# Expert tiles with standing weights: gate and up weights copied by ScalarE, hidden tile made already turned

## The chip, the cores and the metric

The kernel runs on one core of one Trainium2 chip. The metric is the device time of one launch in microseconds, the median of the runs shown.

## The reference

Two transformer layers on 8 sequences of 512 tokens of 256 features, all in float32. Only the last part, a mixture of experts, matters here. Each of the 4096 tokens goes to 4 of 32 experts, chosen by a router; an expert has 128 hidden units:

```python
gate_vals = silu(einsum('th,eih->tei', tokens, gate_w))     # gate_w: 32 x 128 x 256
up_vals = einsum('th,eih->tei', tokens, up_w)
hidden_vals = gate_vals * up_vals
expert_out = einsum('tei,ehi->teh', hidden_vals, down_w)    # down_w: 32 x 256 x 128
sel = take_along_axis(expert_out, topk_idx[:, :, None], axis=1)
mixed = (sel * topk_w[:, :, None]).sum(1)
```

A shared expert and the token itself are added.

## The kernel before

The kernel computes an expert only for the tokens that chose it. Earlier stages (attention of both layers, the first feed-forward, the router) end by scattering each token's row, with its weight and its place, into a table in DRAM that is sorted by expert. The table is cut into pages of 128 rows, one expert a page. All the expert weights wait in SBUF, in `store`, 768 columns per expert: 512 of gate and up (for each half `k` of the 256 features 128 of gate, then 128 of up), then 256 of down.

`pages_of(0, SURE, between)` runs over 136 pages, called expert tiles here, with index `s`. It is written under a manual schedule: each engine executes its instructions in the order of the program, and semaphores between engines are placed by dependencies. One step of the loop does, in this order:

- `fetch(s + 8)`: a DMA on SyncE's queue that brings the rows of a later tile, `r` (L1528).
- `spread(s + 3)`: two TensorE transposes of the rows, `ptr` (L1546), and a VectorE copy out of PSUM to `rT` (L1548).
- `expert_hidden(s + 2)`: the gate and up matmuls `pge` (L1554), with `rT` standing and 256 weight columns per half of the features moving; silu on ScalarE, `acte` (L1558); the product on VectorE, `hide` (L1560), tokens on partitions.
- `turned_hidden(s + 1)`: a transpose of `hide`, `pth` (L1565), and a VectorE copy to `hidT` (L1567).
- `result(s)`: the down matmul `poe` (L1572), with `hidT` standing and 256 columns of `store` moving; ScalarE scales it by the token's weight on its way out of PSUM, `y` (L1574); GpSimd scatters it to DRAM (L944).
- `each(s)`, which is `between`: for finished halves of a sequence pair it issues gathers `z` of four results per token and the VectorE additions (L1602, L1604) into `sums`, spread over 12 of every 16 steps. The last half's additions come three to a step.

Before every eighth tile, `numbers` loads eight experts' numbers from SBUF into registers (L1534), from which TensorE finds the weights in `store`. The number of the buffers of a tag is `bufs`; PSUM has eight banks, two for each of four uses.

After the loop, `rest` holds further pages under conditions that are not taken here, and `complete` gathers and adds the last half and writes it.

Of the kernel before, what the change touches and what calls it, by code (L numbers as in the profile page):

```python
# [12 lines left out]
F32 = mybir.dt.float32  # L13
I32 = mybir.dt.int32
U32 = mybir.dt.uint32
AF = mybir.ActivationFunctionType
ALU = mybir.AluOpType
AX = mybir.AxisListType
PSUM = bass.MemoryType.PSUM
DRAM = bass.MemoryType.DRAM  # L20

P = 128
B, S, H = 8, 512, 256
NT = S // P
NK = H // P
# [781 lines left out]
def _halves(x, u):  # L807

    h, p = divmod(u, B // 2)
    return [x[2 * p + r][:, 2 * h + t, :] for r in range(2) for t in range(2)]  # L810
# [54 lines left out]
def _l1(nc, tc, a, x, out, ident, mhalf, rows, results, filled, inputs, early):  # L865
# [14 lines left out]
    with ExitStack() as ctx:  # L880
        pool = lambda name, bufs, **kw: ctx.enter_context(tc.tile_pool(name=name, bufs=bufs, **kw))
# [14 lines left out]
        for half in range(2):  # L896
            s = slice(half * P, (half + 1) * P)
# [43 lines left out]
        def scatter(group, to, index, source, last):  # L941


            ins = nc.gpsimd.indirect_dma_start(  # L944
                to, bass.IndirectOffsetOnAxis(ap=index, axis=0), source, None, bounds_check=last
            )
            tc.declare_no_dep(ins.ins, group=group, reason="rows are distinct")
            tc.add_to_no_dep_group(group, ins.ins)
            if group == "results":
                tc.declare_no_dep(ins.ins, group="gathers", reason="rows gathered are finished")  # L950
            if group == "rows":
                after(ins, filled)
            scattered[group].append(ins)
            return ins
# [28 lines left out]
        q, k, v, xlT = {}, {}, {}, {}  # L983
        prods, sums, sc, softs, values, turned = {}, {}, {}, {}, {}, {}
# [495 lines left out]
        start = [sum(T[:u]) for u in range(U + 1)]  # L1480
# [17 lines left out]
        store = keep.tile([P, NE, 3 * H], F32, tag="store", name="store")  # L1498
# [20 lines left out]
        routing.close()  # L1519
        tp = pool("m_t", 2)  # L1520
        ps_r = pool("m_psr", 2, space=PSUM)
        ps_t = pool("m_pst", 2, space=PSUM)
        ps_e = pool("m_pse", 2, space=PSUM)
        ps_y = pool("m_psy", 2, space=PSUM)

        def fetch(s):
            r = tp.tile([P, ROW], F32, tag="r", name="r", bufs=TILES + 3)
            ins = nc.sync.dma_start(r, rows[s * P : (s + 1) * P, :])  # L1528
            after(ins, scattered["rows"][-16:])
            return r  # L1530

        def numbers(s):

            _, found = nc.values_load_multi_w_load_instructions(  # L1534
                number[0:1, s : s + 8],
                [mybir.EngineType.PE],
                min_val=0,
                max_val=NE - 1,
                skip_runtime_bounds_check_because="all but the bits of an expert's number are masked out",
            )  # L1540
            return dict(enumerate(found, s))

        def spread(r):
            pt = ps_r.tile([P, S], F32, tag="psr", name="ptr")
            for k in range(NK):
                nc.tensor.transpose(pt[:, k * P : (k + 1) * P], r[:, k * P : (k + 1) * P], ident)  # L1546
            rT = tp.tile([P, H], F32, tag="rT", name="rT", bufs=3)
            nc.vector.tensor_copy(rT, pt[:, :H])  # L1548
            return rT

        def expert_hidden(w, rT):
            pg = ps_e.tile([P, S], F32, tag="pse", name="pge")
            for k in range(NK):
                nc.tensor.matmul(  # L1554
                    pg[:, :H], rT[:, k * P : (k + 1) * P], w[:, k * H : (k + 1) * H], start=k == 0, stop=k == NK - 1
                )
            act = tp.tile([P, P], F32, tag="acte", name="acte", bufs=3)
            nc.scalar.activation(act, pg[:, :P], AF.Silu)  # L1558
            hid = tp.tile([P, P], F32, tag="hide", name="hide", bufs=3)
            nc.vector.tensor_tensor(hid, act, pg[:, P : 2 * P], ALU.mult)  # L1560
            return hid

        def turned_hidden(hid):
            pt = ps_t.tile([P, S], F32, tag="pst", name="pth")
            nc.tensor.transpose(pt[:, :P], hid, ident)  # L1565
            hidT = tp.tile([P, P], F32, tag="hidT", name="hidT", bufs=3)
            nc.vector.tensor_copy(hidT, pt[:, :P])  # L1567
            return hidT

        def result(w, r, hid):  # L1570
            po = ps_y.tile([P, S], F32, tag="psy", name="poe")
            nc.tensor.matmul(po[:, :H], hid, w[:, 2 * H :], start=True, stop=True)  # L1572
            y = tp.tile([P, H], F32, tag="y", name="y", bufs=8)
            nc.scalar.activation(y, po[:, :H], AF.Copy, scale=r[:, H + 1 : H + 2])  # L1574
            scatter("results", results, r[:, H : H + 1].bitcast(U32), y, NTOK * TOPK + NS * P - 1)

        z, sums_of = {}, {}
# [17 lines left out]
        def add(u, t, part):  # L1595

            w, x_t = z[u, t], _halves(x, u)[t]
            if t == 0 and part == 0:
                sums_of[u] = tp.tile([P, NT, H], F32, tag="sums", name="sums", bufs=3)
            to = sums_of[u][:, t, :]  # L1600
            if part == 0:
                nc.vector.tensor_tensor(w[:, :2, :], w[:, :2, :], w[:, 2:, :], ALU.add)  # L1602
            else:
                nc.vector.tensor_tensor(to, x_t if part == 1 else to, w[:, part - 1, :], ALU.add)  # L1604
# [14 lines left out]
        def finish(b, s, last):  # L1619

            sent = scattered["results"][-16:]
            for t in range(NT):
                beside.setdefault(s + 2 + t if last else s + 3 + 3 * t, []).append(partial(gather, b, t, sent))
                for part in range(3):
                    beside.setdefault(s + 5 + 2 * t if last else s + 8 + 3 * t + part, []).append(
                        partial(add, b, t, part)
                    )
            for r in range(2):
                beside.setdefault(s + 8 + 4 * r if last else s + 22 + r, []).append(partial(put, b, (r,)))

        weights = lambda s: store[:, bass.ds(which[s], 1), :].rearrange("p e c -> p (e c)")
        which = {}

        def pages_of(first, end, each):

            tiles, rTs, made, hidTs = {}, {}, {}, {}
            ahead = min(TILES, end - first)
            for s in range(first, first + ahead):
                tiles[s] = fetch(s)
            for s in range(first - 3, end):  # L1640
                if first <= s < end - ahead:
                    tiles[s + ahead] = fetch(s + ahead)
                if s + 3 < end:
                    rTs[s + 3] = spread(tiles[s + 3])
                if first <= s + 2 < end:
                    if (s + 2) % 8 == 0:
                        which.update(numbers(s + 2))
                    made[s + 2] = expert_hidden(weights(s + 2), rTs.pop(s + 2))
                if first <= s + 1 < end:
                    hidTs[s + 1] = turned_hidden(made.pop(s + 1))  # L1650
                if s >= first:
                    result(weights(s), tiles.pop(s), hidTs.pop(s))
                    each(s)

        def between(s):
# [7 lines left out]
        def rest(s):  # L1663

            with tc.If(filled_rows > s * P):
                with tc.manual_schedule():
                    pages_of(s, s + 8, lambda _: None)
                if s + 8 < NS:
                    rest(s + 8)
# [14 lines left out]
        with tc.manual_schedule():  # L1684
            pages_of(0, SURE, between)
            for s in sorted(beside):
                for f in beside[s]:
                    f()
        rest(SURE)

        def complete(units):

            last = [(u, t) for u in units for t in range(NT)]
            for n in range(-4, len(last)):
                if n >= 0:
                    for part in range(3):
                        add(*last[n], part)
                    put(*last[n], nc.scalar)
                if n + 4 < len(last):
                    gather(*last[n + 4], None)  # L1700
# [147 lines left out]
```

## Time and profile before

| | |
|---|---|
| median of 3 runs | 2006.84 us (2006.36 to 2014.84) |
| the profiled execution | 2012.53 us, span 2010.7 us |
| TensorE busy in the span | 1887.2 us (94%) |
| VectorE, ScalarE, GpSimd busy | 1369.8, 1087.6, 1095.5 us |
| mean granted TensorE clock | 0.975 |
| the expert tiles | from 1759 to 1989 us of the span |

Engines are named PE (TensorE's matmuls), PEld (its weight loads), DVE (VectorE), ACT (ScalarE), POOL (GpSimd) and SP (SyncE). A timeline row gives the start in the span, the time to the end of the last of its instructions, the engine, the line, the operation, the tiles (out<-in, names without buffer numbers), the array's rows and columns, the shape and the count; in brackets stands the engine's idle time before it and what ended that. In a windows table, each column is an engine's busy time in that stretch with its instructions in parentheses, then the granted clock (1.00 is full), the mean busy share of the DMA engines and what they moved. A program's f32 matmul appears as two PE instructions, each with a weight load; a transpose as one. A matmul's shown duration includes its way through the array, so that successive ones overlap; the distance of their starts is what a series of them costs.

### The profile page before, as it was taken

To read this page: it belongs to the slowest core of one execution; us is meant where nothing else is said; L and a number is where in the kernel's file an instruction comes from. 1 tells how busy PE (TensorE), PEld (TensorE's weight loads), DVE (VectorE), ACT (ScalarE), POOL (GpSimd) and SP (SyncE) were. 2 spreads that over 40 slices of the span, in tenths; PEclk is the share of its full clock that TensorE was granted. 3 is DMA by queue.
4 is the path that set the end of the run, shared out by engine and by line. 5 is a ranking of instruction groups with operands and counts; after the bars stand their busy time and mean duration, and the time that the engine had idled before them with its cause. 6 is when DMAs were issued, how large, how long until landed. Compare 5 with 4: busy or idle time off the path is not lost. (4 is left out here: it accounts for less than half of the span.)

```text
span 2010.7 us, 48841 instructions
## 1 busy us (share of the span) xinstructions
PE 1887.2 (94%) x17824; PEld 1292.1 (64%) x17824; DVE 1369.8 (68%) x3675; ACT 1087.6 (54%) x2320; POOL 1095.5 (54%) x1294
## 2 busy tenths in 40 slices
PE   7999999999999999999999999989899886899995
PEld 4666676666667666666666666646556544488884
DVE  4677777777777777776777555346887687356666
ACT  3777677777777777777762221235444333144442
POOL 4666786867868678676783110100444444455553
PEclk9999999999999999999999999999999998799998
DMA  8999999999999999999993434910111112747887
GB/s 294 318 310 288 293 297 300 299 298 304 294 304 311 295 306 296 303 283 297 298 311 116 141 121 139 131 21 0 44 44 47 52 49 89 289 150 232 249 259 242
DMA packets 383060, 438.07 MB, mean 218 GB/s; under 512 B 42849, under 2 KB 364385, under 8 KB 382305
## 3 DMA queue, kind: packets, MB, share of 16 engines
q1 hardware_dynamic: 368608, 398.17, 64.7%
q0 software_dynamic: 12672, 35.14, 4.8%
q8 instruction: 146, 2.39, 0.5%
q10 hardware_dynamic: 1536, 1.57, 0.2%
q14 instruction: 98, 0.79, 0.1%
HBM read 235.75 MB, written 199.05 MB: 216 GB/s over the span
## 5 line engine op out<-in xcount | busy, mean ns | idle before, releaser
L448 DVE CUSTOM_DVE_ANT_0 e<-sc,winc 128x512 f32<-128x512 f32 x512 | 333.2, 689 | 280.2 <-PE sc L434 156.6
L451 ACT ACTIVATE e<-e,low 128x512 f32<-128x512 f32 x512 | 365.6, 715 | 96.8 <-DVE low L448 95.7
L372 ACT COPY strip<-pa 128x512 f32<-128x512 f32 x512 | 275.2, 591 | 129.0 <-POOL winc L402 59.2
L375 POOL TENSOR_TENSOR own<-aside,strip 128x512 f32<-128x512 f32 x256 | 269.0, 1051 | 124.9 <-ACT strip L372 108.2
L465 DVE COPY et<-et_ps 128x512 f32<-128x512 f32 x512 | 328.4, 683 | 0.8 <-PE et_ps L462 0.8
L422 PE MATMUL sc<-sm,sm 32*128 32x256 f32 (+3 forms) x1792 | 310.0, 436 | 1.0 <-DVE low L448 0.8
L365 PE MATMUL pa<-pos,sm 32*128 32x256 f32 x2048 | 291.9, 401 | 0.1
L944 POOL DMA_INDIRECT rows<-pay,slot x128 | 148.7, 1162 | 210.7 <-issue 156.8
L402 POOL TENSOR_TENSOR winp<-winp,own 128x256 f32<-128x256 f32 x256 | 187.7, 733 | 98.1 <-DMA winp<-shift 76.2
L422 PEld LDWEIGHTS sc<-sm,sm 32*128 32x128 f32 x1792 | 164.5, 184 | 98.0 <-DVE et L465 35.3
L434 PE MATMUL sc<-ident,winp 128*128 128x128 f32 x1280 | 203.2, 286 | 24.7 <-DMA winp<-shift 24.3
L402 POOL TENSOR_TENSOR winc<-winc,own 128x256 f32<-128x256 f32 x256 | 187.2, 731 | 57.9 <-DMA winc<-shift 46.4
L434 PEld LDWEIGHTS sc<-ident,winp 128*128 128x128 f32 x1280 | 137.1, 142 | 102.4 <-issue 58.3
L944 POOL DMA_INDIRECT results<-y,r x136 | 133.3, 980 | 105.0 <-ACT y L1574 54.7
L462 PE MATMUL et_ps<-ident,e 64*128 64x64 f32 x4096 | 184.4, 230 | 1.1 <-DVE et L465 1.1
L365 PEld LDWEIGHTS pa<-pos,sm 32*128 32x128 f32 x2048 | 176.1, 185 | 10.9 <-ACT strip L372 3.9
L59 POOL TENSOR_TENSOR rstd<-var,mhalf 128x2 f32<-128x2 f32 (+1 forms) x56 | 47.2, 844 | 243.4 <-DVE var L57 235.0
L462 PEld LDWEIGHTS et_ps<-ident,e 64*128 64x128 f32 x4096 | 149.1, 140 | 44.2 <-issue 22.2
L474 PE MATMUL ctx_ps<-et,v 128*32 128x128 f32 x4096 | 167.7, 282 | 0.5 <-DVE et L465 0.5
L1554 PE MATMUL pge<-store,rT 128*128 x544 | 141.3, 382 | 3.1 <-DVE rT L1548 1.4
L739 ACT ACTIVATE hT<-ph,b 128x512 f32<-128x512 f32 x64 | 44.0, 687 | 165.6 <-PE ph L736 165.6
L175 PE MATMUL pq<-xnT,wqk 128*128 128x512 f32 x256 | 132.7, 643 | 0.7 <-PE pv L157 0.7
(227 smaller groups left out, 3200.6 us busy)
## 6 DMA issues: line engine op xcount, KB each, us to landing
shift<-strip SPq DMA_DIRECT2D x256, 510.0 KB
winp<-shift SPq DMA_DIRECT2D x128, 384.0 KB
winc<-shift SPq DMA_DIRECT2D x128, 384.0 KB
winp<-shift SPq DMA_DIRECT2D x128, 256.0 KB
winc<-shift SPq DMA_DIRECT2D x128, 256.0 KB
rows<-empty SPq DMA_DIRECT2D x8, 2640.0 KB
r<-rows SPq DMA_DIRECT2D x136, 132.0 KB
z<-results SPq DMA_DIRECT2D x32, 512.0 KB
```

The lines of the kernel that those rows point to most:

```text
L365: nc.tensor.matmul(pa[:, t * W : (t + 1) * W], src[rs, i * P : (i + 1) * P], pos[rs, g, :], start=True, stop=True)
L372: nc.scalar.copy(st[:, 2 * j : 2 * j + 2, :].rearrange("p t w -> p (t w)"), pas[j])
L375: nc.gpsimd.tensor_tensor(own, aside.unsqueeze(2).to_broadcast([P, 2, 2, P]), st[:, :, W - 1 : W].rearrange("p (j t) o -> p t j o", t=2).t ...
L402: nc.gpsimd.tensor_tensor(dst, dst, own[:, t], ALU.add)
L422: nc.tensor.matmul(sc[:, c0:c1], s[side_][rs, cut : cut + P], s[2 + side_][rs, c0:c1], start=c0 == 0, stop=False, skip_group_check=True,)
L434: nc.tensor.matmul(sc[:, m * P : (m + 1) * P], wins[n + 2 * (m - i)][1][:, j, (i - m + 1) * P : (i - m + 2) * P], ident, start=False, stop ...
L448: nc.vector.tensor_tensor_reduce(e, sc, wins[n][0][:, j, :], 1.0, -LOW, ALU.add, ALU.min, low)
L451: nc.scalar.activation(e, e, AF.Exp, bias=low, scale=-1.0, accum_out=totals[b, g // 2][:, i, r : r + 1])
L462: nc.tensor.transpose(bank[:, c : c + 64], e[rs, m * P : (m + 1) * P], ident[rs, rs])
L465: nc.vector.tensor_copy(et[:, f].rearrange("p j m q -> p (j m q)"), bank)
L474: nc.tensor.matmul(ctx_ps[32 * r : 32 * r + 32, i * P : (i + 1) * P], vs[b % 2][:, m, g % 2, g // 2 * 4 + r, :], et[:, :, m, :], start=m = ...
L944: ins = nc.gpsimd.indirect_dma_start(to, bass.IndirectOffsetOnAxis(ap=index, axis=0), source, None, bounds_check=last)
```

## The change

Gate and up change places with the rows: the weights stand and `rT` moves, so that `pge` comes out with hidden units on partitions, as the down matmul wants it. `turned_hidden` goes, with its PSUM pool and its VectorE copy. The standing weights are no longer addressed in `store` by a register: `brought`, called four tiles ahead and first in the step, has ScalarE copy the 512 columns of the tile's expert into a fixed buffer `w` (one of four). The numbers are now loaded into registers of TensorE (for the down weights) and of ScalarE (for the copies). Results of odd tiles are scaled out of PSUM by VectorE, those of even tiles by ScalarE as before. `y` has 6 buffers instead of 8, `sums` 2 instead of 3, `pge` and `poe` three PSUM banks each instead of two.

```diff
-        ps_t = pool("m_pst", 2, space=PSUM)
-        ps_e = pool("m_pse", 2, space=PSUM)
-        ps_y = pool("m_psy", 2, space=PSUM)
+        ps_e = pool("m_pse", 3, space=PSUM)
+        ps_y = pool("m_psy", 3, space=PSUM)
...
-                [mybir.EngineType.PE],
+                [mybir.EngineType.PE, mybir.EngineType.Activation],
...
         def expert_hidden(w, rT):
             pg = ps_e.tile([P, S], F32, tag="pse", name="pge")
-            for k in range(NK):
-                nc.tensor.matmul(
-                    pg[:, :H], rT[:, k * P : (k + 1) * P], w[:, k * H : (k + 1) * H], start=k == 0, stop=k == NK - 1
-                )
+            for half in range(2):
+                for k in range(NK):
+                    nc.tensor.matmul(
+                        pg[:, half * P : (half + 1) * P],
+                        w[:, k * H + half * P : k * H + (half + 1) * P],
+                        rT[:, k * P : (k + 1) * P],
+                        start=k == 0,
+                        stop=k == NK - 1,
+                    )
...
-        def turned_hidden(hid):
-            pt = ps_t.tile([P, S], F32, tag="pst", name="pth")
-            nc.tensor.transpose(pt[:, :P], hid, ident)
-            hidT = tp.tile([P, P], F32, tag="hidT", name="hidT", bufs=3)
-            nc.vector.tensor_copy(hidT, pt[:, :P])
-            return hidT
-
-        def result(w, r, hid):
+        def brought(s):
+            w = tp.tile([P, 2 * H], F32, tag="w", name="w", bufs=4)
+            nc.scalar.copy(w, store[:, bass.ds(which[s], 1), : 2 * H].rearrange("p e c -> p (e c)"))
+            return w
+
+        def result(s, w, r, hid):
             po = ps_y.tile([P, S], F32, tag="psy", name="poe")
             nc.tensor.matmul(po[:, :H], hid, w[:, 2 * H :], start=True, stop=True)
-            y = tp.tile([P, H], F32, tag="y", name="y", bufs=8)
-            nc.scalar.activation(y, po[:, :H], AF.Copy, scale=r[:, H + 1 : H + 2])
+            y = tp.tile([P, H], F32, tag="y", name="y", bufs=6)
+            if s % 2:
+                nc.vector.tensor_scalar(y, po[:, :H], r[:, H + 1 : H + 2], None, ALU.mult)
+            else:
+                nc.scalar.activation(y, po[:, :H], AF.Copy, scale=r[:, H + 1 : H + 2])
...
-            for s in range(first - 3, end):
+            for s in range(first - 4, end):
+                if s + 4 < end:
+                    if (s + 4) % 8 == 0:
+                        which.update(numbers(s + 4))
+                    brings[s + 4] = brought(s + 4)
                 if first <= s < end - ahead:
                     tiles[s + ahead] = fetch(s + ahead)
-                if s + 3 < end:
+                if first <= s + 3 < end:
                     rTs[s + 3] = spread(tiles[s + 3])
                 if first <= s + 2 < end:
-                    if (s + 2) % 8 == 0:
-                        which.update(numbers(s + 2))
-                    made[s + 2] = expert_hidden(weights(s + 2), rTs.pop(s + 2))
-                if first <= s + 1 < end:
-                    hidTs[s + 1] = turned_hidden(made.pop(s + 1))
+                    made[s + 2] = expert_hidden(brings.pop(s + 2), rTs.pop(s + 2))
                 if s >= first:
-                    result(weights(s), tiles.pop(s), hidTs.pop(s))
+                    result(s, weights(s), tiles.pop(s), made.pop(s))
                     each(s)
```

More of the change, by code (lines that the diff above doesn't have):

```diff
@@ L1598, in add @@
             if t == 0 and part == 0:
-                sums_of[u] = tp.tile([P, NT, H], F32, tag="sums", name="sums", bufs=3)
+                sums_of[u] = tp.tile([P, NT, H], F32, tag="sums", name="sums", bufs=2)
             to = sums_of[u][:, t, :]
@@ L1634, in pages_of @@
         def pages_of(first, end, each):
-            tiles, rTs, made, hidTs = {}, {}, {}, {}
+            tiles, rTs, made, brings = {}, {}, {}, {}
             ahead = min(TILES, end - first)
```

## The prediction

> **What bounds the kernel now.** I read the page's slices first, then the groups of the last 250 us, then one period of the timeline. The change touches only the loop over expert tiles, which starts when the first fetched rows land, at 1759 us, and ends with the last result at 1989. The busy time by windows shows which engine carries it:
>
> ```profile
> core 0: us, PE busy (x) PEld busy (x) DVE busy (x) ACT busy (x) POOL busy (x), PEclk, DMA share, GB/s
> 1757.00:1764.00 7.00, 6.06 (x29) 4.09 (x28) 2.20 (x7) 0.79 (x3) 0.00 (x0) 1.00 0.69 207
> 1764.00:1985.00 221.00, 218.35 (x1188) 181.60 (x1187) 142.08 (x468) 98.74 (x264) 128.55 (x132) 1.00 0.74 227
> 1985.00:2010.70 25.70, 3.48 (x16) 2.13 (x14) 12.90 (x29) 2.45 (x6) 4.74 (x5) 0.66 0.64 228
> ```
>
> TensorE is busy in 218 of 221 us, at the full granted clock; no other engine passes two thirds, and the DMA engines stand at 0.74. A busy TensorE is not proof of a bound, because the ends of matmuls are modelled. So the starts decide, in one period of the timeline:
>
> ```profile
> 1800.55 0.27 PE L1565 MATMUL pth<-ident,hide 128*128 128x128 f32 x1
> 1800.55 0.30 PEld L1572 LDWEIGHTS poe<-store,hidT 128*128 128x128 f32 x2
> 1800.65 0.60 PE L1572 MATMUL poe<-store,hidT 128*128 x2
> 1801.09 0.38 PE L1546 MATMUL ptr<-ident,r 128*128 128x128 f32 x2
> 1801.20 0.73 PEld L1554 LDWEIGHTS pge<-store,rT 128*128 128x128 f32 x4
> 1801.31 1.03 PE L1554 MATMUL pge<-store,rT 128*128 x4
> 1801.51 0.42 DVE L1548 COPY rT<-ptr 128x256 f32<-128x256 f32 x1
> 1802.17 0.27 PE L1565 MATMUL pth<-ident,hide 128*128 128x128 f32 x1
> ```
>
> Start to start: the turn of the hidden tile takes 0.11 us (0.108 in the records), the result 0.44, the two turns of the rows 0.22, gate and up 0.86. The sum, 1.63, is the period: 113 of the 135 intervals between results are 1.63 us. There is no gap between matmuls, so matmuls set the pace. The rest of the 225 us between first and last result is 6.6 us of longer intervals (0.1 to 0.5 us at most loads of the expert numbers, 1.5 us once) less 1.4 us at the end.
>
> Each f32 matmul of the program is two instructions on TensorE, each with a weight load. 256 columns cost 0.217 us ((1.03 - 0.38)/3), 128 columns 0.11 ((0.38 - 0.27)/1).
>
> **Gate and up, and the turn that goes.** Before, rT stands still and 256 weight columns move, four instructions a tile. After, a 128 by 128 piece of weights stands still and 128 columns of rT move: eight instructions, the same number of columns, but eight loads instead of four, each with 0.11 us instead of 0.22 to hide behind. The price depends on how fast loads follow one another. The nearest row has a new full load before each of 16 short matmuls:
>
> ```profile
> 1378.05 1.97 PE L1172 MATMUL pl<-rw,xT 128*128 128x32 f32 x16
> 1378.04 1.86 PEld L1172 LDWEIGHTS pl<-rw,xT 128*128 128x128 f32 x16 [0.33 <-ACT xT L1165]
> ```
>
> The loads start every (1.86 - 0.19)/15 = 0.111 us, though one is shown with 0.19; the matmuls every (1.97 - 0.28)/15 = 0.113. And the two loads of the result start 0.11 apart (0.30 - 0.19) while the 128 columns of pth stream, and the result's matmul starts 0.10 after pth's. So a full load runs under a 128-column matmul. I take 0.111: 8 x 0.111 = 0.89 us, against 0.866 now. The result of this order is already turned (hidden units on partitions), so pth with its 0.108 us goes. Per tile: +0.024 - 0.108 = -0.084; over 136 tiles **-11.4 us**. With the transposes' 0.109 it is -0.102 and -13.9; with 0.113, -0.070 and -9.5. The new period is 1.54.
>
> A rule speaks against this. The Trainium skill, in "TensorE: Matmul & The Clock Gate", Part 3, The mechanism, says that weight loads overlap with matmuls in flight only when their row groups differ. By it, and with the 0.11 us that both take here, the eight pairs would take 8 x 0.22 = 1.76 us and the kernel would lose over 100 us. The rows of pth and poe, both over all 128 rows, contradict it, and I go by them.
>
> **The copies on ScalarE.** One 128x512 copy per tile. From PSUM such a copy takes 0.59 us (strip, L372); from SBUF the trace has 128x1024 at 1.04 (pay, L1157), of which half is 0.52; I take 0.6. Add 0.05 for a register operation (51 to 55 ns on TensorE; none is shown on ScalarE) and a load of eight numbers every eight tiles, 0.79/8 = 0.10. Silu stays at 0.28, and the 0.47 evacuation is left on even tiles, 0.24 a tile. ScalarE goes from 0.75 to 1.27 us of a 1.54 us period. Each copy is issued two steps before its matmuls, and its buffer was last read two steps earlier, so it hides under TensorE: zero. If cover fails, it is because the queue is in order: silu of tile s+2 stands behind the copy of s+4, and a number load delays it by up to 0.9 us; hid is not wanted by TensorE for two more steps, which absorbs it.
>
> **VectorE.** The 0.28 us hidT copy goes from each tile; odd tiles gain an evacuation, 128x256 from PSUM. No such operation is in the trace. The rT copy of that size and source takes 0.42; a 128x256 tensor_scalar between SBUF tiles (L64) takes 0.40 to 1.13, 0.81 in the middle. I take 0.42, because the source is PSUM and rT holds 0.42 beside the same GpSimd scatters. The sum falls, but the order tightens: on odd tiles y, which waits for the result, stands before the next rT, and so does the add (0.42 or 0.68) of a finished half on three of four steps. Laid out by hand, with starts 0.08 earlier than ends as hid and hidT show, rT is then ready 1.56 us into the step where TensorE wants it at 1.76, less 0.2 of signalling: just in time, and late by about 0.2 at 12 steps with an odd tile and a 0.68 add (two per half, six halves), +2.4 at most, 0 at best. I take +0.5.
>
> **Number loads on TensorE.** Same count (17), now two steps earlier in the order than before the turn of rows, and first used four tiles later. They still block TensorE's sequencer for 0.79. At the start the load stood between the first turns and the first gate matmul (1759.0 to 1759.8); now it runs while the rows are awaited: **-0.4**. The others I leave at zero; they lie between -3.7 (all their long intervals go; about that much of the 6.6 stands at them) and +9.7 (fully exposed, 17 x 0.79 less 3.7).
>
> **One answer each.** At the end one turn and one copy leave the chain of the last tile, some 0.7 us, but VectorE's adds run there to 1994.3 us and hide part: -0.4, between 0 and -1. The y buffers fall from 8 to 6: 9.2 us of tiles against 0.75 to the scatter and 2 to 5 us to its landing in the packet records, so nothing waits. Two sums buffers serve units 16 tiles apart: nothing. The first copy waits for the same scatters as the first row fetch, whose landing is later: nothing. Queues of SyncE and GpSimd keep their order.
>
> **Sum.** -11.4 + 0.5 - 0.4 - 0.4 = -11.7. The profiled execution takes 2012.5 us (span 2010.7 and 1.8 around it), 5.7 over the median; it would become 2000.8. The difference carried to the median gives **1995.1 us**.
>
> **Rivals.**
> - *VectorE becomes late* (no change). If y takes 0.81 as in L64's middle, an odd step's rT is ready 0.3 later: every one of the 36 odd steps with an add (six halves of 12 steps, half odd) stalls by 0.13 to 0.4: 24 x 0.13 + 12 x 0.4 = 8 us, leaving -3.7: 2003. For: the in-order queue. Against: PSUM source, and rT unaffected.
> - *Weight loads become the bound* (slower). The place is the eight gate and up pairs; it decides from 0.122 us a pair, since 1.63 - 0.22 - 0.44 = 0.975 = 8 x 0.122. If a load needs the 0.19 us that its row shows before the next may begin, the period is 0.66 + 1.52 = 2.18, +0.55 x 136 = +75: 2082. Even 0.131 gives +10. For: eight loads back to back beside moving matmuls stand nowhere in the trace. Against: 0.111 at L1172 and 0.11 at poe.
> - *The number loads stop costing* with the wait on hid gone, so that the sequencer runs further ahead: up to -3.7 more, 1991.
>
> **How the numbers follow.** My case and the last rival together 0.70; they lie at 1989 to 1998 (-13.9 - 3.7 - 0.4 + 0 gives 1989; -9.5 with +2.4 gives about 1999, part of which counts as no change). VectorE late, or half the gain lost elsewhere: 0.17. Weight loads or another new bound: 0.13. A change of 0.5%, 10 us, is about what a measurement of this kernel can tell. The range runs from 1989 to 2005: it takes in the first case's ends and the VectorE rival, and leaves out the slower one and a little at the bottom. The likeliest case alone spans 1989 to 1999.
>
> **What would show it.** Right: result starts 1.54 us apart; gate and up 0.89 with loads 0.11 apart; ScalarE near 1.27 us a tile; 8 fewer microseconds or more between 1759 and the last result. Wrong: idle TensorE time before pge ended by VectorE's rT; pairs over 0.122; y on VectorE over 0.5; ScalarE's copy over 0.9 us, or silu ending the waits of hid so late that poe waits.

## The result, and the profile after

| | before | changed |
|---|---|---|
| median of 8 runs, same chip | 2010.65 us | 2023.41 us |
| the profiled execution | 2012.53 us, span 2010.7 | 2018.44 us, span 2016.6 |
| first to last result (starts) | 224.8 us | 235.6 us |
| median interval between results | 1.63 us | 1.55 us |
| intervals longer than that, and their excess | 19, 6.5 us | 55, 29.1 us |

The changed kernel is slower: ratio 1.0053, 95% interval 1.0038 to 1.0068 (the two medians alone give 1.0063, inside the interval). That is some 11 us more, where 11.7 us less were predicted. In the profiled executions the span grows by 5.8 us: the loop's first result starts 5.5 us earlier (the stages ahead of it, which are not changed, ended earlier in that execution), the loop takes 10.8 us more, and what follows its last result 0.5 us more. The loop is the change's own: 135 intervals shorter by 0.082 us save 11.1, the long ones cost 22.6 more, and intervals shorter than the median one give 0.8 back.

The busy time by windows of the changed kernel, with the columns of the prediction's first fence:

```profile
core 0: us, PE busy (x) PEld busy (x) DVE busy (x) ACT busy (x) POOL busy (x), PEclk, DMA share, GB/s
1764.00:1985.00 221.00, 203.10 (x1497) 181.41 (x1495) 131.59 (x383) 124.10 (x314) 123.72 (x125) 1.00 0.71 221
```

TensorE is now idle for 18 of 221 us, where it was idle for 2.7. No other engine is near full. The groups of that window say what the changed operations cost, and where the idle time lies (busy time and the mean of one in ns, then the idle time just before them and what ended most of it). First gate and up of the kernel before, in the same window:

```profile
L1554 PE MATMUL pge<-store,rT 128*128 x528 | 137.1, 382 | 2.3 <-DVE rT L1548 1.4 <-issue 0.8
```

Then the changed kernel:

```profile
L1554 PE MATMUL pge<-rT,w 128*128 128x128 f32 x997 | 135.4, 279 | 17.3 <-DVE rT L1547 7.5 <-ACT y L1579 4.0 <-DVE sums L1609 2.8
L1569 ACT COPY w<-store 128x512 f32 x126 | 77.3, 614 | 7.3 <-issue 7.2
L1574 PE MATMUL poe<-store,hide 128*128 x250 | 74.7, 380 | 0.0
L1562 ACT ACTIVATE acte<-pge 128x128 f32<-128x128 f32 x125 | 34.7, 278 | 81.9 <-PE ptr L1545 35.1 <-PE pge L1554 30.5 <-issue 9.8
L1577 DVE TENSOR_SCALAR y<-poe,r 128x256 f32<-128x256 f32 x63 | 30.2, 479 | 1.3 <-PE ptr L1545 0.3 <-issue 0.2 <-PE pge L1554 0.2
```

17.3 us of TensorE's idle time stand before gate and up, where it was 2.3; VectorE's copy of `rT` ends the largest part, and the result never waits. In the timeline one such stall can be followed back:

```profile
1799.76 1.06 PE L1554 MATMUL pge<-rT,w 128*128 128x128 f32 x8
...
1801.08 0.38 PE L1545 MATMUL ptr<-ident,r 128*128 128x128 f32 x2
...
1801.34 1.13 PE L1554 MATMUL pge<-rT,w 128*128 128x128 f32 x8
...
1802.26 0.28 ACT L1562 ACTIVATE acte<-pge 128x128 f32<-128x128 f32 x1 [1.13 <-PE ptr L1545]
...
1802.57 0.29 DVE L1564 TENSOR_TENSOR hide<-acte,pge 128x128 f32<-128x128 f32 x1 [1.38 <-ACT acte L1562]
...
1802.78 0.48 DVE L1577 TENSOR_SCALAR y<-poe,r 128x256 f32<-128x256 f32 x1
1802.94 0.28 ACT L1562 ACTIVATE acte<-pge 128x128 f32<-128x128 f32 x1
...
1803.17 0.41 DVE L1547 COPY rT<-ptr 128x256 f32<-128x256 f32 x1
...
1803.73 1.13 PE L1554 MATMUL pge<-rT,w 128*128 128x128 f32 x8 [0.61 <-ACT y L1579]
```

Read it from the end. Gate and up at 1803.73 waited 0.61 us for `rT`, copied until 1803.58 (the bracket names `y` on ScalarE, which ended 0.01 later and is no input of these matmuls: a wait put down to the event nearest in time). The rows of that copy were turned by 1801.46; the copy stood on VectorE behind an odd `y`, that behind the product `hide`, and that behind a silu that began at 1802.26. ScalarE had idled for 1.13 us before this silu. The matmuls it needs are not those of 1801.34 but those of the tile before, in the first row, which ended at 1799.76 + 1.06 = 1800.82. So the silu came 1.13 us after ScalarE was free and 1.44 after its input was done. The first row also gives the price of a pair: (1.06 - 0.28)/7 = 0.111.

What lies between is TensorE's semaphore, the counter that it raises when a matmul is done and that the next engine waits for; one such update is called a post here. The trace records updates of this semaphore at 1800.74 and then none until 1802.24, where three come 0.04 us apart; the silu begins at 1802.26. Not all posts are recorded: 238 of 536 in the loop before, 317 of 401 after. Before, 95% of the recorded ones lie within 0.06 us of the end of a matmul that posts; after, 59%. The others come up to 0.95 us later, three in one burst 1.8 us later, and often in bursts, 0.043 us apart. A measure that needs no semaphore records is used below: **late silus**, those among 128 tiles (the fifth to the 132nd) that begin over 0.1 us after both the end of their last `pge` matmul and ScalarE's instruction before. The prompt ones begin 0.04 us after. Before: 3 of 128. Changed: 40 of 128.

### The profile page after: what moved, and what is told of

Same layout as the page of the kernel before. It is cut to its first block, busy times and chain, and to the rows that moved or that the text cites. A ratio compares the mean times of both kernels' runs of the same rounds, so it can differ in the third digit from the quotient of the medians.

```text
span 2016.6 us, 49397 instructions
## 1 busy us (share of the span) xinstructions
PE 1876.7 (93%) x18232; PEld 1299.8 (64%) x18232; DVE 1362.8 (68%) x3607; ACT 1120.0 (56%) x2388; POOL 1096.7 (54%) x1294
## 5 line engine op out<-in xcount | busy, mean ns | idle before, releaser
L1554 PE MATMUL pge<-rT,w 128*128 128x128 f32 x1088 | 147.6, 279 | 19.0 <-DVE rT L1547 7.9
L1554 PEld LDWEIGHTS pge<-rT,w 128*128 128x128 f32 x1088 | 132.0, 191 | 28.5 <-ACT y L1579 13.6
```

The lines of the kernel that those rows point to most:

```text
L1554: nc.tensor.matmul(pg[:, half * P : (half + 1) * P], w[:, k * H + half * P : k * H + (half + 1) * P], rT[:, k * P : (k + 1) * P], start=k ...
```

## The experiments

Two theories say why TensorE's posts are late: because full weight loads follow one another without a pause (**spacing**), or because its sequencer, whose register operations and waits the trace lists apart from the matmuls, has nothing to wait for and runs far ahead of them (**run-ahead**). Three rivals do without late posts: ScalarE's copies hold silu back; VectorE's odd `y` holds `rT` back; or the order only lacks slack, a step of spare time between an engine's work and its use. The kernels ran in five groups, A to E, each on one chip together with runs of the kernel before; ratios are against those. Interval is the median one between results, loop is first to last result, excess the sum by which intervals exceed the median one; these and the late silus come from one profiled execution of each kernel, in us.

| run | group | ratio (95%) | interval | loop | excess | late silus |
|---|---|---|---|---|---|---|
| e1 rows stand | A | 0.9987 (0.9966 to 1.0008) | 1.63 | 222.3 | 4.0 | 2 |
| e2 no copies | A | 1.0037 (1.0020 to 1.0054) | 1.55 | 235.6 | 29.2 | 40 |
| e3 y on ScalarE | A | 1.0046 (1.0029 to 1.0064) | 1.55 | 233.6 | 26.7 | 40 |
| e4 result earlier | A | 1.0064 (1.0041 to 1.0088) | 1.65 | 240.6 | 24.4 | 36 |
| e5 wide move | B | 1.0197 (1.0152 to 1.0241) | 1.95 | 260.3 | 0.0 | 0 |
| e6 before, ahead | B | 1.0026 (1.0003 to 1.0049) | 1.63 | 229.0 | 11.2 | 0 |
| e7 turn earlier | B | 0.9996 (0.9972 to 1.0020) | 1.55 | 223.1 | 16.4 | 0 |
| e8 product later | B | 0.9964 (0.9940 to 0.9989) | 1.55 | 212.6 | 5.8 | 0 |
| e9 change again | C | 1.0045 (1.0020 to 1.0069) | 1.55 | 233.1 | 26.6 | 41 |
| e10 product later again | C | 1.0022 (1.0001 to 1.0043) | 1.55 | 230.2 | 23.2 | 42 |
| e11 later, fetch 9 | C | 1.0020 (1.0001 to 1.0039) | 1.55 | 228.5 | 21.8 | 40 |
| e12 turn, fetch 9 | C | 1.0034 (1.0016 to 1.0053) | 1.55 | 231.9 | 24.4 | 35 |
| e13 split before | D | 1.0017 (0.9996 to 1.0038) | 1.65 | 228.9 | 7.0 | 3 |
| e14 wide again | D | one run, 2056.99 us | 1.95 | 260.6 | 0.3 | 1 |
| e15 deep | D | 1.0066 (1.0045 to 1.0086) | 1.55 | 240.8 | 33.9 | 33 |
| e16 before, ahead again | D | one run, 2029.07 us | 1.63 | 231.3 | 13.5 | 6 |
| e17 paced | E | 0.9961 (0.9934 to 0.9989) | 1.55 | 212.4 | 5.8 | 0 |
| e18 rows stand, split | E | 0.9999 (0.9977 to 1.0022) | 1.65 | 225.9 | 4.0 | 0 |

### Parts of the change undone (group A)

e1 gives back the old matmul order, with 256 columns of the copied `w` moving and the hidden tile turned:

```diff
-                        w[:, k * H + half * P : k * H + (half + 1) * P],
-                        rT[:, k * P : (k + 1) * P],
...
+                    pg[:, :H], rT[:, k * P : (k + 1) * P], w[:, k * H : (k + 1) * H], start=k == 0, stop=k == NK - 1
...
+                    made[s + 1] = turned_hidden(made.pop(s + 1))
```

> The matmul order of before (rT stands, 256 columns of the copied w move, the hidden tile is turned again) with the copies on ScalarE and the odd results on VectorE kept. If the loss comes from the eight loads in a row or from TensorE's sequencer running too far ahead (both are gone here): period 1.63 us, TensorE posts prompt, within 4 us of before, either way. If ScalarE's copies delay silu, or the odd results on VectorE delay rT: long periods stay although TensorE's part is that of before, 10 to 20 us slower than before.

In this order the copies and the odd results on VectorE cost nothing: the time is the same as before, with 2 late silus. Its excess of 4.0 us against 6.5 fits the earlier number loads, its other difference from before.

e2 takes the copies away, e3 the odd results on VectorE:

```diff
-                    made[s + 2] = expert_hidden(brings.pop(s + 2), rTs.pop(s + 2))
+                    made[s + 2] = expert_hidden(store[:, (s + 2) % NE, :], rTs.pop(s + 2))
```

> The change without ScalarE's copies: the standing weights are read from store at a fixed expert per tile (number of the tile modulo 32), so gate and up are those of the wrong expert. If ScalarE's copies hold silu back: at least half of the loss against the prediction goes, 1996 to 2003 on before's 2010 scale (7 to 14 us faster than before). If the late posts of TensorE are the cause: silu still starts 0.7 to 1.5 us after pge's end, within 4 us of the changed kernel (6 to 14 slower than before).

```diff
-            if s % 2:
-                nc.vector.tensor_scalar(y, po[:, :H], r[:, H + 1 : H + 2], None, ALU.mult)
-            else:
-                nc.scalar.activation(y, po[:, :H], AF.Copy, scale=r[:, H + 1 : H + 2])
+            nc.scalar.activation(y, po[:, :H], AF.Copy, scale=r[:, H + 1 : H + 2])
```

> The change with all results scaled out of PSUM by ScalarE, none by VectorE. If VectorE's in-order queue (odd y ahead of rT) is the cause: 8 to 22 us faster than the changed kernel, down to the predicted 12 us below before. If TensorE's late posts are the cause: stalls stay, they then come from rT behind a late product alone; between the changed kernel's time and 6 us less.

Both keep 40 late silus and some 27 to 29 us of excess. ScalarE, with nothing but silu and even results in e2, is as late as with copies. Both rivals fall.

e4 makes TensorE wait for the product of the step before:

```diff
-                if s >= first:
-                    result(s, weights(s), tiles.pop(s), made.pop(s))
+                if s + 1 >= first:
+                    result(s + 1, weights(s + 1), tiles.pop(s + 1), made.pop(s + 1))
```

> The change with the result taken one step earlier (result of tile s+1 behind gate and up of s+2), so that TensorE waits for the product of the step before, as before's turn of the hidden tile did, and its sequencer cannot run further ahead than that. If run-ahead causes the late posts: posts become prompt (over 0.85 within 60 ns of a matmul's end), silu follows pge at once, period 1.55 to 1.6, 5 to 12 us faster than before. If eight loads in a row are the cause: silu is as late as in the changed kernel and poe now waits for it too, 10 to 40 us slower than the changed kernel.

36 silus are late, and now the result waits as well (53 of 135 intervals are 1.55, against 77 in the changed kernel, and the mean is 240.6/135 = 1.78 against 1.75); the loss is near the changed kernel's instead of 10 us or more beyond it:

```profile
PE poe L1574 <- DVE hide L1564: 10.0, 24, 1.2
```

(Waits of TensorE: total in us, times, longest.) One more wait a step does not make the posts prompt. It says little on run-ahead, because the wait did not hold the sequencer back: the lead that is measured under D and E is 1.09 us here, against 0.96 in the changed kernel.

### More slack, and a group without late posts (B)

```diff
 # e5: 192 columns move in each pair
-                        pg[:, half * P : (half + 1) * P],
+                        pg[:, half * 192 : half * 192 + 192],
...
-                        rT[:, k * P : (k + 1) * P],
+                        rT[:, k * 64 : k * 64 + 192],
 # e6, on before: turn and result a step later
-                    hidTs[s + 1] = turned_hidden(made.pop(s + 1))
+                    hidTs[s] = turned_hidden(made.pop(s))
...
-                    result(weights(s), tiles.pop(s), hidTs.pop(s))
+                    result(weights(s - 1), tiles.pop(s - 1), hidTs.pop(s - 1))
 # e7: rows turned four tiles ahead, rT bufs=4
-                    rTs[s + 3] = spread(tiles[s + 3])
+                    rTs[s + 4] = spread(tiles[s + 4])
 # e8: VectorE's product behind the next rT
+                if first <= s + 1 < end:
+                    made[s + 1] = product(*made[s + 1])
```

> The change with 192 instead of 128 moving columns in each of the eight gate and up pairs (the extra columns and the shift that they force in the second half of the features are not the model's), so that each load has 0.163 instead of 0.111 us before the next. Pair price then 0.163, period 8 x 0.163 + 0.66 = 1.97 without stalls. If the close spacing of full loads delays TensorE's posts: posts prompt (over 0.9 within 60 ns), every interval 1.97, first to last result 135 x 1.97 = 266 us. If it is the number of instructions in flight: the share of prompt posts stays under 0.75, and long intervals remain here and there.

> Before, with the turn of the hidden tile and the result one step later, so that TensorE never waits for the product of the step before and its sequencer runs as far ahead as in the changed kernel; loads and columns are those of before. If run-ahead delays the posts: fewer than 0.8 of them within 60 ns, silu up to a microsecond behind pge, some intervals over 1.63, 3 to 12 us slower than before. If the eight loads in a row do: posts prompt as in before (0.95), period 1.63, within 3 us of before (about 1 us more at the end of the loop).

> The change with the rows turned one step earlier (four tiles ahead, four rT buffers), so that a late rT has 1.55 us more. If the lag of the posts is bounded by about 1.5 us: it is absorbed, no stalls, every interval 1.55, 10 to 13 us faster than before. If TensorE's posts fall behind at a rate (about 0.7 us a tile while it runs without a stop): the stalls come later but as large, mean period 1.70 to 1.75, within 5 us of the changed kernel.

> The change with VectorE's product of tile s+2 issued one step later, behind the next copy of rT, so that a late silu no longer holds rT back; the result still has a step to spare. If the lag is bounded: most stalls go, 6 to 12 us faster than before. If the posts fall behind at a rate: stalls stay, since the turned rows' own post is late too; within 5 us of the changed kernel.

No kernel of this group has a single late silu, whatever its order, so e5 and e6 tell nothing of the cause, and e7 and e8 nothing of a bound on the lag. e6 is slower than before without a late silu (excess 11.2 us); why is not shown. e8 shows what the loop takes without late posts: 212.6 us, 12.2 less than in the profile of before, where 11.7 were predicted for the change. Its order on VectorE is another than the change's, so this does not confirm the sum; the timed runs gained 7 us (0.9964 of 2018.35, the median of before beside them), with up to 12 inside the interval. e7 turned rows earlier without fetching them earlier, and met a new wait, with intervals of up to 4.5 us every 16 tiles, behind the gathers on SyncE's queue:

```profile
PE ptr L1545 <- DMA r<-rows: 12.2, 8, 2.5
```

### The same kernels beside the change (C)

e9 is the changed kernel and e10 the kernel of e8, unaltered. e11 and e12 fetch nine tiles ahead (`TILES = 9`; e12 with five `y`).

> The changed kernel unaltered, beside the three that follow. If late posts belong to its order of work (nothing between TensorE and the next wait has slack): under 0.7 of the posts within 60 ns again, many intervals of 1.65 to 2.7, 5 to 14 us slower than before. If they were a matter of the run that was profiled: posts prompt, and then 6 to 12 us faster than before, like the kernel with the later product.

> The kernel with the product one step later, unaltered, beside the changed kernel on the same chip. If the order behind rT is what counts: posts prompt again, intervals 1.55 with some 8 us of longer ones, 5 to 11 us faster than before, 12 to 22 faster than the changed kernel. If the earlier run was luck of the chip: it stalls as the changed kernel does, within 4 us of it.

> The kernel with the later product, with rows fetched nine tiles ahead instead of eight. If what is left of its long intervals (ptr waits for rows after gathers have held SyncE's queue) is a matter of the fetch's lead: 1.5 us of lead more take away most of the 3.6 us that ptr waited for rows, 2 to 4 us faster than with eight. If not: the same within 2 us.

> The kernel with the rows turned one step earlier, with rows fetched nine tiles ahead and five y buffers, so that the fetch has the lead that it has in the changed kernel. With eight it lost some 25 us to intervals of 2 to 4.5 us every 16 tiles, where ptr waits for rows. If the missing lead was the cause: those go, loop 211 to 216 us, 6 to 12 us faster than before. If TensorE's posts fall behind at a rate: long intervals stay without a wait for rows, within 5 us of before.

The windows of e8 and then of e10, one kernel in two groups, each with its row of gate and up:

```profile
1764.00:1985.00 221.00, 215.59 (x1638) 196.39 (x1636) 142.88 (x419) 139.43 (x337) 134.35 (x135) 1.00 0.77 240
L1554 PE MATMUL pge<-rT,w 128*128 128x128 f32 x1088 | 144.3, 276 | 0.4 <-DVE rT L1547 0.4
```

```profile
1764.00:1985.00 221.00, 207.03 (x1518) 183.97 (x1518) 127.26 (x377) 122.35 (x312) 122.34 (x122) 1.00 0.70 216
L1554 PE MATMUL pge<-rT,w 128*128 128x128 f32 x1004 | 135.6, 278 | 12.5 <-DVE rT L1547 5.2 <-ACT acte L1562 2.8 <-ACT w L1572 1.8
```

The clock is full in both; in C TensorE starts 120 matmuls fewer, 42 silus are late instead of none, and the loop takes 230.2 us instead of 212.6. The timed runs moved with it, from 0.9964 to 1.0022. So late posts belong to the order of work and to something that differs between occasions; groups A and B ran on a chip of the same number. The traces carry a mark of it that does not depend on late silus: in all six profiles of B and E all but a few posts of TensorE in the loop are recorded (400 of 401 in e8, 533 of 536 in e18), each within 0.015 us of a matmul's end. In the first comparison and in A, C and D 40 to 88% are (238 of 536 before, 327 of 401 in e10, 216 of 536 in e13), and there records of ScalarE's and VectorE's posts are missing too, in every kernel, prompt or late. What makes the occasions differ is not known.

Neither a step more of slack for the product (e10), nor for the rows (e12), nor more lead of the fetch (e11) removes the late posts: the expectation that slack heals the loss fell. The longest delay is not shorter with more slack: 1.6 us in e9, and 2.9, 1.9 and 2.8 in e10 to e12.

### What makes the posts late (D, E)

```diff
 # e13, on before: eight pairs of 128 columns, rT still stands
-                    pg[:, :H], rT[:, k * P : (k + 1) * P], w[:, k * H : (k + 1) * H], start=k == 0, stop=k == NK - 1
...
+                        pg[:, half * P : (half + 1) * P],
+                        rT[:, k * P : (k + 1) * P],
+                        w[:, k * H + half * P : k * H + (half + 1) * P],
...
 # e15: e12 with a third bank for ptr, the result a step later, four hide
-        ps_r = pool("m_psr", 2, space=PSUM)
-        ps_y = pool("m_psy", 3, space=PSUM)
+        ps_r = pool("m_psr", 3, space=PSUM)
+        ps_y = pool("m_psy", 2, space=PSUM)
...
+                    result(s - 1, weights(s - 1), tiles.pop(s - 1), made.pop(s - 1))
```

e14 is e5 and e16 is e6, unaltered.

> Before, with each gate and up matmul cut into two of 128 moving columns, so that there are eight pairs as in the changed kernel, but rT stands, the hidden tile is turned, and nothing else moves. Pair price 0.111: period 1.66, +4 us against before. If a load every 0.11 us without a pause is what delays TensorE's posts: under 0.8 of them within 60 ns, long intervals, 10 to 25 us slower than before. If the changed kernel's order (no wait on the step before) is: posts as in before, 2 to 6 us slower than before.

> The kernel with 192 moving columns once more (its gate and up are not the model's), beside kernels whose posts tell whether this chip delays them at all. If the spacing of loads matters, posts prompt and every interval 1.95 even where the others stall. If it does not: share of prompt posts under 0.75, as in the changed kernel.

> The changed kernel with a step more of slack on both sides of gate and up: rows turned four tiles ahead (four rT, three banks for ptr), the result one step later (four hide, two banks for poe), rows fetched nine ahead, five y. If the lag of the posts stays under its 1.5 us: absorbed, nearly all intervals 1.55, loop 211 to 216 us, 8 to 13 us faster than before. If it grows as long as TensorE runs without a stop: mean period 1.68 to 1.75 here too, 0 to 12 us slower than before.

> Before with the turn of the hidden tile and the result one step later, once more, beside the others. If TensorE's sequencer running ahead delays the posts: under 0.8 of them within 60 ns. If load spacing does: over 0.9, as in before, whatever the chip.

This group has late posts (e15: 33 silus), so the others speak. e13 runs more matmuls a microsecond than the changed kernel (13 in 1.65 us against 12 in 1.55, each with its load), eight of them with loads 0.11 us apart, and has 3 late silus:

```profile
L1555 PE MATMUL pge<-store,rT 128*128 x997 | 132.7, 276 | 2.0 <-DVE rT L1548 0.9 <-DMA r<-rows 0.8
```

2.0 us idle before gate and up, against 17.3 in the changed kernel. **Spacing alone falls.** Pairs of 192 columns (e14) have 1 late silu here, and before with everything a step later (e16) has 6; the kernel before itself has no profile in this group. e15, with the most slack of all, is the slowest, with 1.78 us a tile on average and delays of up to 2.7 us: the lag is not a fixed one that a pipeline step absorbs. A part of its loss is its own, since TensorE also waits 5.9 us for the fewer `poe` banks to be read:

```profile
PE poe L1574 <- DVE y L1577: 5.9, 11, 0.7
```

The traces also show how far the sequencer runs ahead. Before each result it does a register operation that finds the down weights in `store`; its lead is the time from the start of that operation to the start of the result's first weight load (median of the same 128 tiles). It is 0.78 us before and 0.96 in the changed kernel. In group D it is 0.81 in e13, 2.06 in e14, 1.29 in e16 and 1.59 in e15. So **run-ahead alone falls** as well: e14 has the longest lead, its loads are 0.16 us apart, and 1 silu is late. Of these four only e15 has close loads and a long lead together. Even the two together are not enough on every occasion: e7 and e8 have loads 0.11 us apart and leads of 2.09 and 1.37 us, and not one late silu.

The last two were to part the sequencer's load from its waits. e17 gives it more register operations again (an offset of zero, made from the expert's number); e18 is e1 with eight pairs, none with a register operation.

```diff
 # e17
+            zero = number // NE * P
...
-                        rT[:, k * P : (k + 1) * P],
+                        rT[:, P:] if k else rT[:, bass.ds(zero, P)],
 # e18
-                    pg[:, :H], rT[:, k * P : (k + 1) * P], w[:, k * H : (k + 1) * H], start=k == 0, stop=k == NK - 1
...
+                        pg[:, half * P : (half + 1) * P],
+                        rT[:, k * P : (k + 1) * P],
+                        w[:, k * H + half * P : k * H + (half + 1) * P],
```

> The changed kernel with one thing added: the moving rT of the first half of the features is addressed by a register (an offset that is always zero, made from the expert's number), so that TensorE's sequencer has a register operation before each half of gate and up, three a tile as before instead of one. If its running ahead without anything to do is what delays the posts: over 0.85 of them within 60 ns, intervals 1.55 with few long ones, 6 to 13 us faster than before and 14 to 24 faster than the changed kernel's place of 9 to 10 behind before. If the eight standing weights themselves or the missing wait on the hidden tile are: under 0.7, 5 to 14 us slower than before.

> The kernel in which rT stands again and the copied w moves (copies and odd results kept, hidden tile turned), with its gate and up cut into eight pairs of 128 columns: eight loads 0.11 us apart, no register operation among them, but TensorE waits for the hidden tile before its turn. If the sequencer without register operations is the cause: under 0.75 within 60 ns, 8 to 20 us slower than before. If the waits of before keep it in step: over 0.88 as in the split before, period 1.65, 1 to 6 us slower than before.

Neither has a late silu, which fits several theories, and the changed kernel was not run beside them; since group B shows that whole groups go without late posts, they settle nothing on the cause. e17's gate and up and its loop:

```profile
L1557 PE MATMUL pge<-rT,w 128*128 x544 | 106.6, 278 | 0.4 <-DVE rT L1549 0.4
```

0.4 us idle, and 212.4 us from first to last result (the sequencer's lead is 1.05 us). With 0.9961 it is the fastest version beside before, as e8 was in B; e8 lost in C, and e17 was not run where posts are late.

**What stays open:** what holds TensorE's posts back, and why in some groups only. It came with the changed order (standing weights, no turn, few register operations), in groups A, C and D and in the first profile; the copies, the odd results, the spacing alone, run-ahead alone and the lack of a step of slack are excluded. Close loads and run-ahead together, on such an occasion, fit all runs; that they are the cause is not shown, since the standing weights and the missing turn, which part e15 from e13 too, fit as well. Whether the changed kernel itself would gain in a group like B was not tried.

## Why the prediction was wrong, step by step

- **Gate and up, and the turn: right.** Pairs start 0.1116 us apart (0.111 predicted), the interval is 1.55 (1.54). The median interval is 1.55 in every kernel of this order with 128 moving columns but e4. The rival in which weight loads become the bound is out: it needed 0.122. The Trainium skill's rule that weight loads overlap only where row groups differ ("TensorE: Matmul & The Clock Gate", Part 3, The mechanism) does not describe these loads: they all span 128 rows, and eight of them run at 0.1116 us each under moving matmuls.
- **Copies: right.** 0.614 against 0.6, and e2 without them loses as much.
- **VectorE: the size of `y` was near** (0.479 for 0.42), and e3 shows that it is not the cause. The failing step stands in the sentence after it: `rT` "just in time, and late by about 0.2 at 12 steps", "less 0.2 of signalling", priced at +0.5 and at most +2.4. The long intervals cost 22.6 us more. The layout by hand had ScalarE and VectorE begin on TensorE's work as promptly at every step as in the period that it was read from; in 40 of 128 tiles silu began 0.26 to 2.2 us later than its input and its engine allowed.
- **"hid is not wanted by TensorE for two more steps, which absorbs it": failed.** It is true of the result, which never waited (0.0 us). But the late product stands before the next `rT` on VectorE, and `rT` has no step to spare. The prediction followed the queue for the odd `y` and the additions, not for a product that waits.
- **The rival "VectorE becomes late"** named the place where the time is lost, and a price of 8 us for a mechanism that does not act; undoing its premise (e3) left 40 late silus and 26.7 us of excess. None of the rivals on record held what the runs show, late posts from TensorE.
- **Number loads:** e1, with the old order and the earlier loads, has 2.5 us less excess than before had on another occasion, inside the range given (-3.7 to +9.7); no run changes the loads alone.
- **The tail:** +0.5 after the last result instead of -0.4.
- **What was listed as a sign of being wrong** showed: idle TensorE before `pge` ended by `rT`. The other signs (pairs over 0.122, `y` over 0.5, copy over 0.9, a waiting result) did not.

## What to carry to other kernels

A period worked out from the starts of matmuls is the floor of a loop, not its time: for each wait that TensorE meets, write down the whole chain back to TensorE's own post, through every instruction that stands before it in the queues of ScalarE and VectorE, and ask what a post one microsecond late would do to it. When an engine idles before an instruction whose inputs have long ended, compare the end of the input with the start, tile by tile: that separates a late signal from a slow engine, where the profile's releaser names whatever ended nearest. And compare a kernel with itself on another occasion before a gain of half a per cent is believed: e8 and e10 are the same kernel.

## What the runs showed of the hardware

- TensorE's semaphore posts can come long after the matmul they follow: in the changed kernel 41% of those recorded in the loop were over 0.06 us late, up to 0.95 us and once 1.8, several of them then 0.043 us apart, while the recorded ones of ScalarE and VectorE came within 0.013 us. The matmuls themselves went on at 0.1116 us a pair meanwhile, so the matmul rows do not show it; the next engine's idle time does.
- The same kernel shows it on one occasion and not on another (42 late silus and none), at the same granted clock of 1.00. On the occasions without it the trace also holds nearly every record of TensorE's posts (400 of 401 in the loop for e8, 327 of 401 for e10). What connects the two is not known.
- TensorE's sequencer can run 2.1 us ahead of its matmuls with every post prompt (e7), so a long lead by itself does not delay posts.
- Full 128 by 128 weight loads of float32 run at one per 0.1116 us under 128-column matmuls for a whole loop, and a pair of 192 columns costs 0.05 more ((1.95 - 1.55)/8).
